# A decoder layer on one core: early score groups subtract earlier, VectorE evicts some queries, late rows are moved, and the last block takes other PSUM banks

## The chip, the cores and the metric

The kernel runs on one core of a Trainium2 chip. The metric is the device time of the whole program in microseconds; less is better. One execution was taken by the hardware profiler, and every view below is of that execution.

## The reference, cut to what matters

There are 16 sequences of 256 tokens with 256 features, all in float32 (4,096 token rows).

1. **First attention.** Rows are normalised, four heads of 64 features are multiplied with 256 fixed keys, the scores go through relu and square, and the result is multiplied with fixed values: `y = x + out`, then a layer norm of `x + y`.
2. **Cross attention.** 16 heads of 16 features attend within each sequence to 256 rows of a context. The logits have a bias that depends on a clipped difference of two scalars per row: `attn = q·k + ap_h * max(D,0) + an_h * min(D,0)`, with `D = clip(frac_k - frac_q, -0.2, 0.2)`. Softmax, values, an output projection, a residual, a layer norm.
3. **Feed-forward.** 256 to 1,024 to 256 features with relu, and a low-rank correction (rank 4) that one of eight experts adds, chosen by a gate. A residual and a last layer norm.

## The kernel before, in words

The order of all instructions is written out by hand (`manual_schedule`), and each engine runs its own instructions strictly in that order. The rows are held as 8 blocks of 512.

**First stage, up to about 259 us:** the first attention, block after block.

**Second stage, from about 259 to 840 us:** one loop over `n` from 0 to 65. Each `n` below 64 is a *group*: one sequence (batch `b = n // 4`) and four of its heads (`og = n % 4`). The work of a group is spread over three rounds of the loop. Its names and lines:

- `negative` (L588 on GpSimd, L593 on ScalarE) makes `an_h * dneg` for the four heads of group `n+1`, `count` of them on GpSimd and the others on ScalarE, into a tile `neg` (three buffers).
- `positive` (L600, ScalarE) writes `ap_h * dpos` into the four PSUM banks `ps_l`, and `logits` (L609, TensorE, 16 matmuls) adds `q·k` to them.
- `maxima` (L624, VectorE, eight instructions) adds `neg` and the bank, stores the sum in `neg` and keeps each row's maximum `mx`.
- `subtract` (L639) takes the maxima off: heads 0 and 1 on GpSimd, heads 2 and 3 on VectorE. Both read two SBUF tensors (`neg`, `mx`).
- in round `n+1`: `turned` (L649, TensorE transposes, four matmuls a head) and `exps` (L656, ScalarE), heads 0 and 1 first, then a *large piece*, then heads 2 and 3.
- in round `n+2`: `attend` (L665, TensorE) and, every second group, `keep` (L678, VectorE copies the bank `av`); after a batch's last group the sums and values leave by DMAs (L521, L529), are inverted (`invert`, L537, VectorE) and spread by DMAs (`spread`, L539, L547).

The large piece depends on `og`: 0 is `queries` of the next batch (L437, evicted at L447 by ScalarE), 1 is `project` of an older batch (L561, added at L570 by VectorE), 2 is `keys` (L457, evicted at L467 by VectorE and copied by eight DMAs, L473, into `kM`), 3 is `vals` (L479, evicted at L487 by VectorE into `vaug`) with a *small piece* behind heads 2 and 3: the transposes L424 of the batch after next.

`tile_b` hands out three PSUM banks in strict rotation to all of these: heads 0 to 3 of `turned`, the large piece, the small piece. So an allocation waits until the one three before it has been evicted.

From `n = 15` on (`FIRST`), the feed-forward of one block is laid into eight rounds (`part` 0 to 7, the block's `ff`). Part 0 turns the rows, part 1 has the matmuls of the gate (L764, copied at L772), parts 2 and 3 (`halved`) have half of the inner products each (L830, L842, relu at L849 on ScalarE and L853 on VectorE) and, in part 2, `route` (L783 to L799, VectorE), and parts 4 to 7 have the outer products (L860). Rounds 0 to 14 have no `ff`; they are called *early groups* here.

Before the change, `subtract` stands behind the eviction of the large piece:

```python
if older:
    older.keep()
...
step(large_piece)
...
if now and not halved:
    now.subtract((nc.gpsimd, nc.gpsimd if n == 0 else nc.vector))
```

The second half of the first attention's last block is finished in rounds 24 to 27: one `norm_out` (L249 on ScalarE, L379 on GpSimd) at the end of each.

**End, from about 840 us:** blocks `six` and `seven` of the feed-forward without groups beside them. `six.inner(1)` uses the four banks `ps_l` again, behind their relu of the first half (L849, L853).

Of the kernel before, what the change touches and what calls it, by code (L numbers as in the profile page):

```python
# [10 lines left out]
AF = mybir.ActivationFunctionType  # L11
ALU = mybir.AluOpType
AX = mybir.AxisListType

P = 128
# [6 lines left out]
def tile_decoder_layer(ctx: ExitStack, tc: tile.TileContext, a: dict, out: bass.AP):  # L22


    nc = tc.nc
    NTOK, C = a["x"].shape
    B, S = a["frac"].shape
    NT = NTOK // P
    NB = NTOK // 512
# [67 lines left out]
    bq_s = const.tile([P, CC], FP, name="bq_s")  # L97
# [10 lines left out]
    loraB = const.tile([P, F], FP, name="loraB")  # L108
# [278 lines left out]
    if True:  # L387
# [8 lines left out]
        class Batch:  # L396
# [33 lines left out]
                self.xT = p2.tile([P, CC, S], FP, tag="xT", bufs=1, name="xT")  # L430
                nc.scalar.copy(self.xT.rearrange("p c t -> p (c t)"), ps)

            def queries(self):
                ps = tile_b()
                for o in range(CC):
                    for c in range(CC):
                        nc.tensor.matmul(  # L437
                            ps[:, o * S : (o + 1) * S],
                            lhsT=wq[:, c, o * P : (o + 1) * P],
                            rhs=self.xT[:, c, :],  # L440
                            start=(c == 0),
                            stop=(c == CC - 1),
                        )
                yield
                self.qT = p2.tile([P, CC, S], FP, tag="qT", name="qT")
                for o in range(CC):
                    nc.scalar.activation(  # L447
                        self.qT[:, o, :], ps[:, o * S : (o + 1) * S], AF.Identity,
                        bias=bq_s[:, o : o + 1], scale=qscale,
                    )  # L450
# [236 lines left out]
        def pieces(n):  # L687

            b, og = divmod(n, 4)
            ahead, nxt, last, older = (  # L690
                batches[b + d] if 0 <= b + d < B else None for d in (2, 1, -1, -2)
            )
            if og == 0:
                return nxt and nxt.queries(), None, []
            later = nxt if nxt and nxt.b >= MADE else None
            if og == 1:
                return older and older.project(), None, [later and (lambda: later.clip("dneg"))]
            if og == 2:
                return nxt and nxt.keys(), None, [later and (lambda: later.clip("dpos"))]
            more = [ahead and ahead.load]  # L700
            if ahead:
                more.append(ahead.reload if ahead.b < MADE else ahead.fractions)
            return nxt and nxt.vals(), ahead and ahead.turned(), more
# [7 lines left out]
    if True:  # L711
        out_view = out.rearrange("(b j p) c -> b p j c", j=4, p=P)

        class Block:
# [99 lines left out]
                self.umT = pm.tile([P, 512], FP, tag="umT", bufs=1, name="umT")  # L814
                nc.scalar.copy(self.umT, ps)

            def inner(self, half, gs=range(4)):
                if half == 0 and 0 in gs:
                    if self.tb == NB - 1:
                        h0 = pm.tile([P, 4, 512], FP, tag="pT", name="hT0")  # L820
                        h1 = p2.tile([P, 4, 2, S], FP, tag="neg", bufs=3, name="hT1")
                        self.hT = [h0[:, g] for g in range(4)]
                        self.hT += [h1[:, g].rearrange("p j k -> p (j k)") for g in range(4)]
                    else:
                        h = pm.tile([P, FC, 512], FP, tag="hT", bufs=1, name="hT")
                        self.hT = [h[:, f] for f in range(FC)]
                for g in gs:
                    f = 4 * half + g
                    for c in range(CC):
                        nc.tensor.matmul(  # L830
                            banks[g],
                            lhsT=wi[:, c, f * P : (f + 1) * P],
                            rhs=self.xT[:, c, :],
                            start=(c == 0),
                            stop=False,
                        )

            def lora(self, half, scalar=(0, 2)):
                for g in range(4):
                    f = 4 * half + g  # L840
                    rows = slice(ER * g, ER * g + ER)
                    nc.tensor.matmul(  # L842
                        banks[g], lhsT=loraB[rows, f * P : (f + 1) * P], rhs=self.umT[rows, :],
                        start=False, stop=True,
                    )
                for g in range(4):
                    f = 4 * half + g
                    if g in scalar:
                        nc.scalar.activation(  # L849
                            self.hT[f], banks[g], AF.Relu, bias=wib[:, f : f + 1]  # L850
                        )
                    else:
                        nc.vector.tensor_scalar(  # L853
                            self.hT[f], banks[g], wib[:, f : f + 1], 0.0, ALU.add, ALU.max
                        )

            def outer(self, j, ps):
# [15 lines left out]
                nc.vector.tensor_tensor(rows, rows, ps[:, 0:C], ALU.add)  # L873
                row_stats(rows, self.mv[:, j, :])

            def finish(self, j):
                ps = tile_b()
                self.outer(j, ps)
                self.add(j, ps)

# [14 lines left out]
    with tc.manual_schedule():  # L895
# [15 lines left out]
        by = [None] * (NB + 1)  # L911
# [4 lines left out]
        for tb in range(NB):  # L916
            now = rows_in[tb]
# [29 lines left out]
            if tb + 1 < NB:  # L947
                nxt = rows_in[tb + 1]
# [50 lines left out]
        banks = [psL.tile([P, 512], FP, tag=f"L{g}", name=f"ps_l{g}") for g in range(4)]  # L999
# [8 lines left out]


        FUSED, FIRST = NB - 2, 15  # L1010
        six, seven = rows_out[NB - 2 :]
        rest = rows_in[NB - 1]
        rest.mv = const.tile([P, 4, 2], FP, name="mv_rest")
        for n in range(N + 2):
            now, nxt, last, older = (
                groups[n + d] if 0 <= n + d < N else None for d in (0, 1, -1, -2)
            )
            large_piece, small_piece, more = pieces(n)
            tb, part = divmod(n - FIRST, 8)
            ff = rows_out[tb] if 0 <= tb < FUSED or (tb == FUSED and part < 2) else None  # L1020
            halved = ff and part in (2, 3)
# [15 lines left out]
            if older and not halved and n != N:  # L1037
                older.attend()
            if nxt:
                nxt.negative(4 if 1 <= n < FIRST - 1 else 3)  # L1040
            if prep:
                prep.root()
            if done:
# [13 lines left out]
            if halved:  # L1057
                for g in range(2):
                    last.turned(g)
                    last.exps(g)  # L1060
                if part == 2:
                    ff.route()
                now.subtract((nc.gpsimd, nc.vector))
                if part == 2:
                    ff.biased()
                if done:
                    done.ready(newton(done.mv, done.near, 4))
                ff.inner(part - 2, range(0, 3))
                if part == 2:
                    ff.turn_um()  # L1070
                ff.inner(part - 2, range(3, 4))
                ff.lora(part - 2, scalar=(0,))
                for g in range(4):
                    nxt.positive(g)
                older.attend()
            else:
                if nxt:
                    nxt.positive(0)
                    nxt.positive(1)
                if last:  # L1080
                    last.turned(0)
                    last.exps(0)
                if nxt:
                    nxt.positive(2)
                if last:
                    last.turned(1)
                    last.exps(1)
                if n == N:
                    older.attend()
                if nxt and not (ff and part == 0):  # L1090
                    nxt.positive(3)
                if prep:
                    prep.rows()
            if older:
                older.keep()
            if n == 0:
# [18 lines left out]
            divided = batches[b - 2] if og == 0 and b >= 2 else None  # L1115
            if divided and ff:
                divided.divide()
            if now and not halved:
                now.subtract((nc.gpsimd, nc.gpsimd if n == 0 else nc.vector))
            if divided and not ff:  # L1120
                divided.divide()
            if done and not halved:
# [15 lines left out]
                    extra()  # L1138
            if 16 <= n < 20:
                row_stats(rest.y[:, n - 16, :], rest.mv[:, n - 16, :])  # L1140
            if 24 <= n < 28:
                rest.norm_out(by[NB], n - 24, n - 24, nc.gpsimd)

            tb, part = divmod(n - FIRST + 4, 8)
            if part < 3 and 0 <= tb <= FUSED:
# [13 lines left out]
        six.inner(0, range(3, 4))  # L1159
        six.lora(0)  # L1160
        end.divide()
        six.inner(1)
        step(add)
        step(add)
        six.lora(1)
        for j in range(2, 4):
            seven.measure(j)
        seven.norm()
        six.finish(0)
        six.finish(1)  # L1170
        seven.turn()
        seven.biased()
# [88 lines left out]
```

## Time and profile before

| what | value |
|---|---|
| median of 3 runs | 914.74 us (914.54 to 915.02) |
| the profiled execution's own time | 914.93 us |
| its span in the profile | 913.1 us |
| TensorE busy | 892.4 us (98%) |
| VectorE busy | 707.7 us (78%) |
| ScalarE busy | 584.2 us (64%) |
| GpSimd busy | 379.5 us (42%) |
| granted TensorE clock | 1.0 |

How to read it: an engine's busy time is the union of its instructions' times; the ends of matmuls are modelled. The execution's own time is 1.8 us more than the span. A line of the timeline has the start, the duration, the engine, the source line, the operation, what it writes and reads, how many instructions were merged, and in brackets how long the engine stood idle before it and what ended that. Idle gaps under 0.15 us are not listed.

### The profile page before, as it was taken

The numbers are of one execution on the slowest core, as the hardware profiler recorded it, in microseconds if no ns is written. First come the engines' busy times: TensorE is split into PE (matmuls) and PEld (weight loads), VectorE is DVE, ScalarE is ACT, GpSimd is POOL, SyncE is SP. The second block draws the span as 40 slices with busy tenths as digits, with TensorE's granted clock in tenths as the row PEclk, the third lists the DMA queues.
The fourth block names the chain that finished last, engine by engine and source line by source line (L and its number), as shares of the span: only waits on it lengthen the run. The fifth ranks groups of instructions, "written<-read, shape, count | busy, mean of one in ns | idle before, by whom it ended". The sixth has DMA issues, their size and how long they took to land.

```text
span 913.1 us, 19025 instructions
## 1 busy us (share of the span) xinstructions
PE 892.4 (98%) x6910; PEld 541.6 (59%) x6910; DVE 707.7 (78%) x1968; ACT 584.2 (64%) x977; POOL 379.5 (42%) x369
## 2 busy tenths in 40 slices
PE   6999999999999999999999999999999999999997
PEld 2333333333356776577658757865875686586555
DVE  5788899889878998778777877777787787678443
ACT  4757877787687879466666856665685567556111
POOL 1002312231469996434635543463454336244010
PEclk9999999999999999999999999999999999999999
DMA  5411011100001222010111202011120201111001
GB/s 137 146 36 35 30 36 41 65 1 2 3 11 50 70 71 56 13 42 21 35 43 39 52 13 66 18 37 41 40 52 14 65 17 40 41 27 45 23 1 47
DMA packets 44190, 37.01 MB, mean 41 GB/s; under 512 B 14912, under 2 KB 40000, under 8 KB 44096
## 3 DMA queue, kind: packets, MB, share of 16 engines
q1 hardware_dynamic: 43536, 35.52, 14.0%
q8 instruction: 55, 0.90, 0.4%
q14 instruction: 39, 0.32, 0.1%
q10 hardware_dynamic: 560, 0.26, 0.1%
HBM read 21.07 MB, written 6.03 MB: 30 GB/s over the span
## 4 chain that ended last, share of the span: by engine, by line
PE 56%; ACT 4%; DVE 1%; issue 1%; ACTq 0%; DVEq 0%
PE ps_b L860 12%; PE ps_l L830 12%; PE ps_b L649 9%; PE ps_l L609 6%; PE ps_v L665 5%; PE ps_b L561 3%; PE ps_b L457 2%; PE ps_b L479 2%; PE ps_l L842 2%; ACT ps_l L600 2%; ACT pT L656 1%; PE ps_b L437 1%; PE ps_b L749 1%; ACT qT L447 1%; DVE neg L624 1%
## 5 line engine op out<-in xcount | busy, mean ns | idle before, releaser
L588 POOL TENSOR_SCALAR neg<-dneg,aneg,delta 128x512 f32<-128x512 f32 x205 | 175.7, 869 | 211.2 <-ACT pT L656 185.8
L624 DVE CUSTOM_DVE_ANT_0 neg<-ps_l,neg 128x256 f32<-128x256 f32 x512 | 181.6, 420 | 43.0 <-PE ps_l L609 39.8
L600 ACT ACTIVATE ps_l<-dpos,apos_d 128x512 f32<-128x512 f32 x256 | 173.1, 686 | 34.5 <-DVE mx L624 30.5
L656 ACT ACTIVATE pT<-ps_b 128x512 f32<-128x512 f32 x256 | 143.3, 590 | 59.1 <-PE ps_b L649 57.4
L324 DVE TENSOR_TENSOR pr<-r 128x1024 f32<-128x1024 f32 x128 | 155.5, 1255 | 32.4 <-ACT r L322 32.1
L322 ACT ACTIVATE r<-ps_a 128x1024 f32<-128x1024 f32 x128 | 126.5, 1022 | 59.1 <-PE ps_a L314 33.9
L649 PE MATMUL ps_b<-ident,neg 128*128 128x128 f32 x1024 | 140.3, 278 | 4.0 <-ACT pT L656 2.4
L649 PEld LDWEIGHTS ps_b<-ident,neg 128*128 128x128 f32 x1024 | 112.9, 140 | 41.9 <-issue 15.3
L639 POOL TENSOR_TENSOR neg<-neg,mx 128x1024 f32<-128x1024 f32 x65 | 124.3, 1914 | 30.0 <-DVE mx L624 24.0
L314 PE MATMUL ps_a<-xnT,kT 64*64 64x512 f32 x1024 | 124.2, 601 | 0.0
L334 PE MATMUL ps_v<-pr,vv 64*64 64x512 f32 x1024 | 123.5, 593 | 0.3
L860 PE MATMUL ps_b<-wof,hT 128*128 128x256 f32 x512 | 115.8, 380 | 0.0
L830 PE MATMUL ps_l<-xt,wi 128*128 128x512 f32 x256 | 115.0, 596 | 0.8 <-ACT hT L849 0.8
L860 PEld LDWEIGHTS ps_b<-wof,hT 128*128 128x128 f32 x512 | 96.4, 190 | 16.0 <-issue 2.3
L639 DVE TENSOR_TENSOR neg<-neg,mx 128x1024 f32<-128x1024 f32 x63 | 90.9, 1443 | 0.3
L349 POOL TENSOR_TENSOR xt<-xt,half 128x512 f32<-128x512 f32 x15 | 23.7, 1583 | 141.0 <-ACT half L348 141.0
L334 PEld LDWEIGHTS ps_v<-pr,vv 64*64 64x64 f32 x1024 | 38.1, 132 | 70.7 <-issue 43.7
L314 PEld LDWEIGHTS ps_a<-xnT,kT 64*64 64x64 f32 x1024 | 38.1, 135 | 67.9 <-issue 56.2
L830 PEld LDWEIGHTS ps_l<-xt,wi 128*128 128x128 f32 x256 | 46.8, 190 | 52.0 <-issue 45.8
L609 PE MATMUL ps_l<-kM,qT 32*128 32x256 f32 x1024 | 74.8, 401 | 0.4 <-ACT ps_l L600 0.4
L665 PE MATMUL ps_v<-pT,vaug 128*32 128x256 f32 x1024 | 69.8, 385 | 0.8 <-ACT pT L656 0.8
L853 DVE TENSOR_SCALAR hT<-ps_l,wib 128x512 f32<-128x512 f32 x44 | 30.5, 745 | 42.8 <-PE ps_l L842 42.8
(107 smaller groups left out, 966.9 us busy)
## 6 DMA issues: line engine op xcount, KB each, us to landing
cT<-in_ctxT SPq DMA_DIRECT2D x16, 256.0 KB
kM<-keys SPq DMA_DIRECT2D x128, 32.0 KB
v<-raw SPq DMA_DIRECT2D x128, 32.0 KB
invs<-rows SPq DMA_DIRECT2D x128, 32.0 KB
x<-in_x SPq DMA_DIRECT2D x7, 512.0 KB
out<-x SPq DMA_DIRECT2D x7, 512.0 KB
frow<-in_frac SPq DMA_DIRECT2D x16, 128.0 KB
wi<-in_wiT SPq DMA_DIRECT2D x1, 1024.0 KB
```

The costliest lines, as they stand in the source:

```text
L314: nc.tensor.matmul(sc[64 * k : 64 * k + 64, h, :], lhsT=kT[64 * h : 64 * h + 64, q, hf * P + 64 * k : hf * P + 64 * k + 64], rhs=self.xnT[ ...
L324: nc.vector.tensor_tensor(pr, r, r, ALU.mult)
L334: nc.tensor.matmul(self.acc[k][64 * h : 64 * h + 64, :], lhsT=vv[64 * k : 64 * k + 64, hf, 64 * q : 64 * q + 64], rhs=pr[64 * k : 64 * k + ...
L588: nc.gpsimd.tensor_scalar(self.neg[:, g], self.batch.dneg, aneg[:, h : h + 1], delta, ALU.mult, ALU.mult,)
L600: nc.scalar.activation(banks[g], self.batch.dpos.rearrange("p j k -> p (j k)"), AF.Copy, scale=apos_d[:, h : h + 1],)
L609: nc.tensor.matmul(banks[g][:, j * S : (j + 1) * S], lhsT=self.batch.qT[rows, self.o, j * P : (j + 1) * P], rhs=self.batch.kM[rows, self.i ...
L624: nc.vector.tensor_tensor_reduce(out=self.t[:, g, j, :], in0=banks[g][:, j * S : (j + 1) * S], in1=self.neg[:, g, j, :], scale=1.0, scalar ...
L639: eng.tensor_tensor(rows, rows, top.to_broadcast([P, 4, S]), ALU.subtract)
L649: nc.tensor.transpose(ps[:, k * S + j * P : k * S + (j + 1) * P], self.t[:, g, j, k * P : (k + 1) * P], ident,)
L656: nc.scalar.activation(self.pT[:, g, :], self.ps[g], AF.Exp)
L830: nc.tensor.matmul(banks[g], lhsT=wi[:, c, f * P : (f + 1) * P], rhs=self.xT[:, c, :], start=(c == 0), stop=False,)
L860: nc.tensor.matmul(ps[:, 0:C], lhsT=self.hT[f][:, j * P : (j + 1) * P], rhs=wof[:, f, :], start=(f == 0), stop=(f == FC - 1),)
```

## The change

- Rounds 0 to 14: `subtract` stands directly behind `maxima` and what follows it in the round's first half, ahead of `keep`, of `invert` and of the large piece's eviction. From round 15 on it stays where it was.
- `negative`: in rounds 1 and 2 GpSimd makes three heads and ScalarE one (before: four and none); in parts 0 and 1 GpSimd makes four (before: three and one).
- `queries` of rounds 16, 24, ... 56 are evicted by VectorE instead of ScalarE. These rounds are part 1.
- The four `norm_out` stand at the ends of rounds 24, 27, 28 and 29.
- At the end `six.inner(1)` takes two of its four banks from `tile_b`, and `six.finish(0)` takes the bank `V`.

```diff
-            def queries(self):
+            def queries(self, vector=False):
...
                 for o in range(CC):
+                    if vector:
+                        nc.vector.tensor_scalar(
+                            self.qT[:, o, :], ps[:, o * S : (o + 1) * S], qscale,
+                            bq_s[:, o : o + 1], ALU.mult, ALU.add,
+                        )
+                        continue
                     nc.scalar.activation(
...
-                return nxt and nxt.queries(), None, []
+                return nxt and nxt.queries(n > 15 and n % 8 == 0), None, []
...
-            def inner(self, half, gs=range(4)):
+            def inner(self, half, gs=range(4), own=()):
+
+                if 0 in gs:
+                    self.banks = list(banks)
...
+                    if g in own:
+                        self.banks[g] = tile_b()
...
-            def finish(self, j):
-                ps = tile_b()
+            def finish(self, j, ps=None):
+                ps = ps or tile_b()
...
+        LATE = 24, 27, 28, 29
...
-                nxt.negative(4 if 1 <= n < FIRST - 1 else 3)
+                nxt.negative(4 if 3 <= n < FIRST - 1 or (ff and part < 2) else 3)
...
+            if now and not halved and not ff:
+                now.subtract((nc.gpsimd, nc.gpsimd if n == 0 else nc.vector))
             if older:
                 older.keep()
...
-            if now and not halved:
-                now.subtract((nc.gpsimd, nc.gpsimd if n == 0 else nc.vector))
+            if now and not halved and ff:
+                now.subtract((nc.gpsimd, nc.vector))
...
-            if 24 <= n < 28:
-                rest.norm_out(by[NB], n - 24, n - 24, nc.gpsimd)
+            if n in LATE:
+                j = LATE.index(n)
+                rest.norm_out(by[NB], j, j, nc.gpsimd)
...
-        six.inner(1)
+        six.inner(1, own=(0, 1))
...
-        six.finish(0)
+        six.finish(0, tile_v())
```

(In `inner` and `lora`, `banks[g]` becomes `self.banks[g]`.)

More of the change, by code (lines that the diff above doesn't have):

```diff
@@ L828, in inner @@
                     f = 4 * half + g
+                    if g in own:
+                        self.banks[g] = tile_b()
                     for c in range(CC):
                         nc.tensor.matmul(
-                            banks[g],
+                            self.banks[g],
                             lhsT=wi[:, c, f * P : (f + 1) * P],
@@ L842, in lora @@
                     nc.tensor.matmul(
-                        banks[g], lhsT=loraB[rows, f * P : (f + 1) * P], rhs=self.umT[rows, :],
+                        self.banks[g], lhsT=loraB[rows, f * P : (f + 1) * P], rhs=self.umT[rows, :],
                         start=False, stop=True,
@@ L849, in lora @@
                         nc.scalar.activation(
-                            self.hT[f], banks[g], AF.Relu, bias=wib[:, f : f + 1]
+                            self.hT[f], self.banks[g], AF.Relu, bias=wib[:, f : f + 1]
                         )
@@ L853, in lora @@
                         nc.vector.tensor_scalar(
-                            self.hT[f], banks[g], wib[:, f : f + 1], 0.0, ALU.add, ALU.max
+                            self.hT[f], self.banks[g], wib[:, f : f + 1], 0.0, ALU.add, ALU.max
                         )
```

## The prediction

> **What bounds the kernel now.** I read the busy times first, then TensorE's waits, early groups and the rest apart, then the timeline of single rounds.
>
> ```profile
> PE 892.4 (98%) x6910; PEld 541.6 (59%) x6910; DVE 707.7 (78%) x1968; ACT 584.2 (64%) x977; POOL 379.5 (42%) x369
> ```
>
> TensorE (PE) stands idle for 913.1 - 892.4 = 20.7 us. Its waits are short lists (total us, times, longest), first for 250 to 300 us, then from 335 us on; before 250 us there is only the start, 8.6 us, which the change doesn't touch.
>
> ```profile
> PE ps_b L649 <- ACT pT L656: 1.6, 4, 0.5
> PE ps_l L609 <- ACT ps_l L600: 0.4, 1, 0.4
> ```
>
> ```profile
> PE ps_b L649 <- ACT qT L447: 1.4, 6, 0.2
> PE ps_b L649 <- ACT pT L656: 0.9, 2, 0.4
> PE ps_v L665 <- ACT pT L656: 0.8, 1, 0.8
> PE ps_l L830 <- ACT hT L849: 0.8, 1, 0.8
> PE ps_b L809 <- DVE um L799: 0.5, 1, 0.5
> ```
>
> That is 6.4 us, and all that the edits could win. Everywhere else PE runs without a gap, so whatever makes PE wait anew is added in full. So I ask of each edit whom it makes late. Round 7 (og 3, `vals`) decides:
>
> ```profile
> 300.77 1.15 PE L609 MATMUL ps_l<-kM,qT 32*128 32x256 f32 x16
> 301.01 3.89 POOL L588 TENSOR_SCALAR neg<-dneg,aneg,delta 128x512 f32<-128x512 f32 x4 [0.51 <-POOL neg L639]
> 304.82 0.69 DVE L678 COPY raw<-ps_v 128x512 f32<-128x512 f32 x1
> 304.86 1.89 POOL L639 TENSOR_TENSOR neg<-neg,mx 128x1024 f32<-128x1024 f32 x1
> 305.70 0.69 DVE L487 COPY vaug<-ps_b 128x512 f32<-128x512 f32 x1 [0.20 <-PE ps_b L479]
> 306.31 1.52 DVE L639 TENSOR_TENSOR neg<-neg,mx 128x1024 f32<-128x1024 f32 x1
> 306.47 0.63 PE L424 MATMUL ps_b<-ident,hid 128*128 128x128 f32 x4
> ```
>
> Write L for the start of a round's logits (300.77). Maxima end at L + 4.13 (304.90). `keep` and the eviction of `vals` run while GpSimd subtracts; the eviction ends at 306.39, and L424, which by the rotation takes that bank, starts 0.08 us later, at L + 5.70. The logits of round 8 are queued behind L424. Round 8 (og 0) has nothing between maxima and subtract, so it already is what the change makes of every early group:
>
> ```profile
> 310.69 1.88 POOL L639 TENSOR_TENSOR neg<-neg,mx 128x1024 f32<-128x1024 f32 x1
> 311.21 2.45 DVE L639 TENSOR_TENSOR neg<-neg,mx 128x1024 f32<-128x1024 f32 x1
> ```
>
> VectorE's subtract takes 2.45 us here, 2.26 in round 4 and 2.44 in round 12. Clear of GpSimd's it takes 1.22 (round 15, at 356.87). It ends 1.08 us behind GpSimd's (313.66 against 312.57): it waited.
>
> **The change, part by part.**
>
> **The early subtract.** GpSimd's four negatives may start at L + 0.25 (301.01; 313.08 in round 9, L 312.83) and last 0.76 each, 3.0 together; only the first was stretched, by the previous subtract of VectorE. So GpSimd subtracts from L + 3.3 to L + 5.2, ahead of VectorE, which asks at L + 4.13 and ends at L + 5.2 + 1.08 = L + 6.3. If the previous subtract ends after L + 0.25, this is up to 0.15 later. `keep` and the eviction of `vals` follow, 2 x 0.69 - 0.08 = 1.3: L + 7.6, where L424 wanted L + 5.7. Queued behind that wait on PE are L424 and the next logits; behind the logits, all else. Cost 1.9 us in rounds 7 and 11 each. In round 3 VectorE's previous subtract ends near 276.8, the negatives at 279.75, GpSimd's subtract at 281.6, VectorE's at 282.7, the eviction at 284.0; L424 stood at 282.59, behind 0.53 us of idle that this takes up: 1.4 us. Sum 5.2. If the two subtracts did not meet, the eviction would end at L + 4.13 + 1.22 + 1.3 = L + 6.6, and the cost would be 0.9, 0.9 and 0.2: 2.0. If GpSimd began only at the maxima's end, as at 304.86, it is 2.6, 2.6 and 2.0: 7.2. I take 5.2, since rounds 4, 8 and 12 show the meeting each time.
>
> [...]
>
> **The same edit in the other early groups.** Round 13 (`project`): subtract to L + 6.3, `keep` and L570 to L + 7.5, then two row statistics (1.16 from 343.77 to 344.93): L + 8.6. The next logits come at L + 5.85 and maxima could start 1.29 behind them, L + 7.1: 1.5 late, where they were 0.5 late before (344.89 against 343.12 + 1.29); the exps and transposes hang on them, so PE loses 1.0. Round 9, without statistics: 0.3. Rounds 6, 10 and 14 (`keys`): at most 0.3 late, covered by the stalls of 7 and 11 or by the small vector operations of 14; I take 0. Their eight DMAs to `kM`, and the sums, values and inverses that SP issues, start up to 2.2 us later; the first half of `kM` of round 10 was there about 1.7 us before the logits that read it (330.74), and round 11's stall adds 1.9: covered. Without that stall it costs 0.5. Won back: round 4's wait (0.25) and round 13's (0.44), since after a stall VectorE is on time. Early groups in all: 5.2 + 1.0 + 0.3 - 0.7 = 5.8.
>
> **Negatives.** Rounds 1 and 2 take 0.75 us each off GpSimd. ScalarE's extra 0.72 lies in an idle 1.8 us in round 1; in round 2 it has 0.31 idle, so positives come 0.4 late and PE waits 0.25 (inside the 1.4 of round 3). In parts 0 and 1 GpSimd has idle time of 0.8 to 3.3 us before its instructions (358.28, 361.38, 438.71), so one more is hidden; without it, 0.75. ScalarE's 0.75 less is no one's wait.
>
> **Queries on VectorE** (rounds 16 to 56, six times). Head 3's transposes wait for the bank of the queries:
>
> ```profile
> 445.63 0.66 PE L649 MATMUL ps_b<-ident,neg 128*128 128x128 f32 x4 [0.23 <-ACT qT L447]
> ```
>
> VectorE can evict when the matmuls end (443.8, its maxima end at 442.95): two at 0.44 to 0.49 (L467, same shape and source), done by 444.3 instead of 445.57. The wait goes: -1.4 in all. Behind it on VectorE, divide and subtract end 0.7 us later; then VectorE has 2.1 us idle before the next maxima, so that is hidden. Bounds: -1.4 and 0.
>
> **Late rows.** The one at the end of round 24 stays, and it is its GpSimd addition (447.48) that is queued ahead of round 25's negatives and its subtract (450.43), which `route` meets (L791, 1.66 instead of some 0.35). So the 0.5 us at L809 stays. The other three move to rounds with idle GpSimd and ScalarE: 0. Bounds: -0.85 (round 25 lasts 15.35 between logits, round 33 14.50) and 0.
>
> **Other banks at the end.**
>
> ```profile
> 851.04 7.13 PE L830 MATMUL ps_l<-xt,wi 128*128 128x512 f32 x16 [0.76 <-ACT hT L849]
> ```
>
> The wait goes, the rotation's banks are free (evicted by 844.4), and banks 2 and 3 are free (851.8) before their turn, 3.4 us in: -0.8.
>
> **Sum:** +5.8 - 1.4 - 0.8 = +3.6. From the profiled 914.93 (span 913.1) 918.5; the profiled run lies 0.2 above the median, so 918.3 against 914.74.
>
> **The rivals.**
>
> *Faster: the eviction of `vals` is not awaited.* If L424's bank were another one, late evictions would cost nothing, and the early waits of rounds 3, 4, 13 and 14 (0.4 each but for round 4) would go: -1.5 - 1.4 - 0.8 = -3.7, 911.0. It decides if L424 starts before L487 ends. Against it: the rotation counted out (L424 is three allocations behind `vals`), and L424 starting 0.08 us behind the eviction.
>
> *No change: the subtracts don't meet.* VectorE gets through first, the `vals` rounds cost 2.0, the rest of the early groups nets -0.3 (0.7 won, some 0.4 lost in rounds 9 and 13): 2.0 - 0.3 - 2.2 = -0.5, 914.2; with round 25 gaining, 913.4. It decides if VectorE's subtract lasts under 1.4 us in rounds 5 to 13. For it: round 1, where VectorE went ahead of the fourth negative, which then took 1.73 instead of 0.77. Against it: GpSimd is ready 0.8 us earlier.
>
> *Worse: the chain of SP.* If `kM` lands late in rounds 8 and 12 as well (2.2 us later against 2.3 and 1.7 spare) and the subtracts meet as at 304.86, it is 7.2 + 1.3 + 0.5 - 0.7 - 2.2 = +6.1, 920.8. It decides if PE waits for a DMA there.
>
> **How the numbers follow.** Forecast 0.60, worse 0.13, no change 0.14, faster 0.13. What differs by less than 0.2% (1.8 us) I call the same, about what this measurement can tell. Slower is forecast and worse, 0.73; faster is the first rival and the end of the second, 0.14; same 0.13. The range leaves out about a tenth at each end: 912.6 to 921.0; the forecast's own range is 916.5 to 919.5 (its bounds of 0.85 at round 25, and 0.5 to 1 on the `vals` rounds).
>
> **What would show it.** Right: PE waits at L424 for `vaug` in rounds 3, 7 and 11, 1.4 to 2 us each; VectorE's subtract near 2.3 us in the early groups; no wait for `qT`, none at the end's L830; the wait at L809 still there. Wrong: no listed wait for `vaug`, or subtracts of 1.2 us. A span from first logits to round 15's logits that is shorter than 89.7 us (259.73 to 349.46) would overturn the forecast.

## The result, and the profile after

| | before | after |
|---|---|---|
| median of six runs | 914.64 us (913.71 to 915.02) | 918.00 us (916.14 to 918.40) |
| ratio | | 1.0034, 95% interval 1.0023 to 1.0045 |
| the profiled execution | 914.93 us, span 913.1 | 918.4 us, span 916.6 |

The change made the kernel 3.4 us slower; 918.3 had been predicted. The engines' busy times of the changed kernel:

```profile
PE 892.8 (97%) x6910; PEld 542.2 (59%) x6910; DVE 712.2 (78%) x1980; ACT 573.9 (63%) x955; POOL 380.5 (42%) x379
```

TensorE did the same work in the same busy time (892.4 before), so the 3.5 us by which the span grew are idle time, and matmuls that ran slowly (below). TensorE's waits, whole run (total us, times, longest):

```profile
PE ps_b L424 <- DVE vaug L493: 5.1, 3, 1.8
PE ps_b L655 <- ACT pT L662: 2.3, 5, 0.8
...
PE ps_b L815 <- DVE um L805: 0.5, 1, 0.5
```

The first line is new: three waits for the eviction of `vals` (L493; L487 before). The lines for `qT` (1.4) and `hT` (0.8) are gone, and the wait at `um` stayed. Round 7 in the timeline of the changed kernel; L645 is `subtract`, L684 `keep`:

```profile
304.99 1.89 POOL L645 TENSOR_TENSOR neg<-neg,mx 128x1024 f32<-128x1024 f32 x1
305.88 2.09 DVE L645 TENSOR_TENSOR neg<-neg,mx 128x1024 f32<-128x1024 f32 x1
307.89 0.68 DVE L684 COPY raw<-ps_v 128x512 f32<-128x512 f32 x1
308.49 0.68 DVE L493 COPY vaug<-ps_b 128x512 f32<-128x512 f32 x1
309.22 0.66 PE L424 MATMUL ps_b<-ident,hid 128*128 128x128 f32 x4 [1.65 <-DVE vaug L493]
```

VectorE's subtract asks at 305.88 and ends at 307.97, which is 1.09 behind the end of GpSimd's (306.88). `keep` and the eviction follow, and L424 starts 0.05 behind the eviction's end. This round's logits began at 301.59, so the eviction ends 7.58 behind them: the prediction said 7.6.

At the end, the inner products of the second half now start with a bank of the rotation, straight behind the low-rank part (L853), where 0.76 us of waiting had been:

```profile
853.43 1.14 PE L853 MATMUL ps_l<-umT,loraB 32*128 32x512 f32 x8
854.50 3.70 PE L841 MATMUL ps_b<-xt,wi 128*128 128x512 f32 x8
```

One thing was not foreseen. Busy time in three stretches of 3.41 us (columns: stretch, length, busy us and count of PE, PEld, DVE, ACT, POOL, then the granted TensorE clock, the DMA share and GB/s):

```profile
306.93:310.35 3.42, 1.77 (x18) 1.34 (x22) 2.23 (x3) 1.95 (x4) 2.60 (x4) 1.00 0.19 49
310.35:313.76 3.41, 3.41 (x31) 1.49 (x24) 2.21 (x13) 1.49 (x3) 1.09 (x2) 0.50 0.25 63
334.24:337.65 3.41, 1.82 (x20) 1.40 (x24) 2.58 (x5) 2.00 (x4) 2.70 (x4) 1.00 0.20 48
```

Behind the wait of round 7 the granted clock is 0.50 for 3.41 us, and round 8's matmuls take longer (the logits 1.62 us instead of 1.15). Behind the wait of round 11 (last line) it stays at 1.00.

Where the time went, from the starts of the logits in the two traces (after less before; change within the stretch):

| stretch | us | predicted |
|---|---|---|
| up to the first logits | -0.54 | 0 |
| rounds 3, 7, 11 (`vals`) | +1.21, +1.95, +1.77 = +4.93 | +5.2 |
| round 8 (the clock) | +1.49 | 0 |
| the other early rounds | +1.04 | +0.6 |
| rounds 16, 24, ... 56 (the *gate rounds*) | 6 x -0.45 = -2.70 | -1.4 |
| the other rounds from 15 on | +0.07 | 0 |
| the end | -0.83 | -0.8 |
| sum | +3.46 | +3.6 |

The prediction's test, first logits to round 15's logits, gave 97.19 us against 89.73: longer, as forecast.

The table explains the profiled execution and not all six. Their spans are 916.6, 916.2, 915.2, 915.1, 914.4 and 914.9 us. The granted clock has a mean of 0.997 in the first two, and of 0.999 or 1.0 in the others. Two of the others took 918.03 and 918.01 us all the same, 2.9 and 3.1 us more than their spans, where the profiled one took 1.8 more. No run shows what that extra time is.

### The profile page after: what moved, and what is told of

Its sections match the earlier page's. It is cut to its first block, busy times and chain, and to the rows that moved or that the text cites. A ratio compares the mean times of both kernels' runs of the same rounds, so it can differ in the third digit from the quotient of the medians.

```text
span 916.6 us, 18997 instructions
## 1 busy us (share of the span) xinstructions
PE 892.8 (97%) x6910; PEld 542.2 (59%) x6910; DVE 712.2 (78%) x1980; ACT 573.9 (63%) x955; POOL 380.5 (42%) x379
## 4 chain that ended last, share of the span: by engine, by line
PE 84%; DVE 9%; ACT 3%; issue 2%; DMA 1%; SPq 1%; DVEq 0%; ACTq 0%
PE ps_b L871 11%; PE ps_l L841 11%; PE ps_b L655 11%; PE ps_v L334 10%; PE ps_a L314 10%; PE ps_l L615 7%; PE ps_v L671 6%; PE ps_b L567 3%; DVE pr L324 3%; PE ps_b L437 2%; PE ps_b L485 2%; PE ps_b L463 2%; DVE neg L630 2%; PE ps_l L853 2%; PE ps_b L295 1%
## 5 line engine op out<-in xcount | busy, mean ns | idle before, releaser
L645 POOL TENSOR_TENSOR neg<-neg,mx 128x1024 f32<-128x1024 f32 x65 | 124.4, 1914 | 30.5 <-DVE mx L630 29.7
L314 PE MATMUL ps_a<-xnT,kT 64*64 64x512 f32 x1024 | 123.5, 598 | 0.3 <-ACT r L322 0.3
L871 PE MATMUL ps_b<-wof,hT 128*128 128x256 f32 x496 | 112.3, 380 | 0.0
L841 PE MATMUL ps_l<-xt,wi 128*128 128x512 f32 x248 | 111.5, 595 | 0.0
L871 PEld LDWEIGHTS ps_b<-wof,hT 128*128 128x128 f32 x496 | 93.4, 190 | 15.0 <-issue 1.5
L645 DVE TENSOR_TENSOR neg<-neg,mx 128x1024 f32<-128x1024 f32 x63 | 93.9, 1491 | 0.7
L314 PEld LDWEIGHTS ps_a<-xnT,kT 64*64 64x64 f32 x1024 | 37.9, 134 | 67.8 <-issue 56.2
```

What stands on the lines that cost most here:

```text
L314: nc.tensor.matmul(sc[64 * k : 64 * k + 64, h, :], lhsT=kT[64 * h : 64 * h + 64, q, hf * P + 64 * k : hf * P + 64 * k + 64], rhs=self.xnT[ ...
L645: eng.tensor_tensor(rows, rows, top.to_broadcast([P, 4, S]), ALU.subtract)
L841: nc.tensor.matmul(self.banks[g], lhsT=wi[:, c, f * P : (f + 1) * P], rhs=self.xT[:, c, :], start=(c == 0), stop=False,)
L871: nc.tensor.matmul(ps[:, 0:C], lhsT=self.hT[f][:, j * P : (j + 1) * P], rhs=wof[:, f, :], start=(f == 0), stop=(f == FC - 1),)
```

## The experiments

Every ratio is to the kernel before, measured beside it on the same chip; its medians there were 914.94, 914.92 and 914.84. "Stage" is the time from the first logits to round 15's logits in the profiled execution (before: 89.73). It is the finest measure here: the start of the run alone shifts the first logits by up to 1 us either way between executions, and the stage leaves that out.

| label | median us | ratio, 95% interval | stage us |
|---|---|---|---|
| late_subtract | 910.27 | 0.9951, 0.9938 to 0.9963 | 89.00 |
| early_subtract_only | 920.23 | 1.0057, 1.0045 to 1.0070 | 94.90 |
| vals_first | 913.36 | 0.9983, 0.9974 to 0.9992 | 91.04 |
| queries_only | 911.64 | 0.9969, 0.9956 to 0.9981 | 89.72 |
| negatives_only | 913.95 | 0.9991, 0.9981 to 1.0000 | 89.09 |
| other_bank | 915.10 | 1.0006, 0.9997 to 1.0015 | 93.59 |
| one_input | 927.17 | 1.0137, 1.0120 to 1.0154 | 105.62 |
| late_one_input | 926.50 | 1.0127, 1.0112 to 1.0142 | 104.52 |
| two_pieces | 915.05 | 1.0003, 0.9993 to 1.0012 | 93.98 |
| late_two_pieces | 911.13 | 0.9963, 0.9951 to 0.9976 | 89.86 |
| stall_steps | 918.67 (one run) | | 96.10 |
| after_again | 920.15 (one run) | | 98.27 |

### Which edit costs, and which gain

**late_subtract.** The early subtract undone, all else kept:

```diff
-            if now and not halved and not ff:
-                now.subtract((nc.gpsimd, nc.gpsimd if n == 0 else nc.vector))
...
-            if now and not halved and ff:
-                now.subtract((nc.gpsimd, nc.vector))
+            if now and not halved:
+                now.subtract((nc.gpsimd, nc.gpsimd if n == 0 else nc.vector))
```

> The changed kernel with one edit undone: in rounds 0 to 14 subtract stands behind the large piece's eviction again. The other four edits stay. Theory (the early subtract costs all the loss, the rest only gains): the three waits of PE at L424 for vaug go, the granted clock stays at 1.0 near 310 us, the stage from first logits to round 15's logits is 89.7 us again, and the gate rounds and the end keep their gains, 6 x 0.45 = 2.7 and 0.8: 914.6 - 3.5 = 911.1 us. If the gate rounds are worth only the listed idle of 0.23 each, as predicted, and round 2's three negatives cost 0.25: 914.6 - 1.4 - 0.8 + 0.25 = 912.7. Rival (the loss comes from the negatives or from the moved rows, not from the subtract): it stays near 918.

Measured 910.27, better than both kernels. The waits at L424 and the clock's fall are gone (mean clock 0.999). Its gain by place: -0.73 in the stage, -2.70 in the gate rounds, -0.82 at the end. The -0.73 was not expected; it is round 3, 0.84 shorter, less round 2, 0.11 longer.

**early_subtract_only.** The kernel before, with that one move:

```diff
+            if now and not halved and not ff:
+                now.subtract((nc.gpsimd, nc.gpsimd if n == 0 else nc.vector))
             if older:
                 older.keep()
```

> The kernel before with the early subtract alone. Theory (GpSimd's and VectorE's subtracts exclude each other, so vals' eviction is late and PE waits at L424): waits for vaug of 1.4 to 2 us in rounds 3, 7 and 11, VectorE's subtract near 2 us, first logits to round 15's logits 95.7 us, and 914.6 + 6.0 = 920.6 us; with a fall of the granted clock in round 8, as in the profile of the changed kernel, 97.2 and 922.1. If that fall belongs to the wait, it comes again here; if it is chance, it need not. Rival (the subtracts don't meet; the loss came from the fewer negatives on GpSimd in rounds 1 and 2 that shifted the phase): 916.5 or less.

Measured 920.23, stage +5.17. The waits in rounds 7 and 11 are there (+1.94, +1.76), but round 3 costs only +0.19, where the changed kernel has +1.21. Round 3 in this kernel's timeline:

```profile
280.39 1.28 DVE L639 TENSOR_TENSOR neg<-neg,mx 128x1024 f32<-128x1024 f32 x1
...
282.29 1.89 POOL L639 TENSOR_TENSOR neg<-neg,mx 128x1024 f32<-128x1024 f32 x1
282.93 0.66 PE L424 MATMUL ps_b<-ident,hid 128*128 128x128 f32 x4 [0.83 <-DVE vaug L487]
```

Here VectorE went ahead of GpSimd's subtract and needed 1.28 us. GpSimd came later, since in this kernel it still makes four negatives in round 2. In the changed kernel it makes three, is ready sooner, goes first, and VectorE takes 2.26. Two edits that look unrelated decide together who goes first. The clock stayed at 1.0 behind round 7's wait of 1.65 us: round 8's logits took 1.15.

**vals_first.** The changed kernel, with the subtract behind the eviction again where the large piece is `vals`:

```diff
-            if now and not halved and not ff:
+            if now and not halved and not ff and og != 3:
...
-            if now and not halved and ff:
-                now.subtract((nc.gpsimd, nc.vector))
+            if now and not halved and (ff or og == 3):
+                now.subtract((nc.gpsimd, nc.gpsimd if n == 0 else nc.vector))
```

> The changed kernel, but in early groups with og 3 (rounds 3, 7, 11) subtract stands behind the eviction of vals again; in the other early groups it stays early. Theory (only the eviction of vals is awaited by PE): the three waits at L424 go (5.0 us by the listed idle) and, if the clock's fall near 310 us hangs on the wait of round 7, that goes too (1.5); what is left of the early edit is +1.0 (round 13 with its row statistics), so 914.6 + 1.0 - 2.7 - 0.8 = 912.1 us, first logits to round 15's logits 90.8. Rival (the early subtracts of og 0 to 2 push the later evictions by themselves, through queries and keys): waits stay at other pieces, 915 or more.

Measured 913.36 (912.1 expected), stage +1.31. No wait at L424, no fall of the clock (mean 0.999). What is left: +0.94 in round 9, +0.44 and +0.68 in rounds 13 and 14, and -0.84 won in round 3. The early move costs in the `project` rounds too, and the most that it wins in any round is 0.15 (round 12).

**queries_only.**

```diff
-                return nxt and nxt.queries(), None, []
+                return nxt and nxt.queries(n > 15 and n % 8 == 0), None, []
```

> The kernel before with one edit: queries of rounds 16, 24, ... 56 are evicted by VectorE. Theory A (the wait of PE for qT is really 0.45 each, since the listed idle begins only at the modelled end of the matmuls before it): 914.6 - 2.7 = 911.9 us, each of the six rounds 0.45 shorter. Theory B (0.23 each, the listed idle, as predicted; the rest of the gain in the changed kernel came from the negatives that left ScalarE in the same rounds): 914.6 - 1.4 = 913.2.

Measured 911.64; each of the six rounds is 0.45 shorter, so theory A. Round 16 in its timeline, evicted by VectorE (L448), then the transposes of heads 2 and 3 and the logits:

```profile
364.12 1.00 DVE L448 TENSOR_SCALAR qT<-ps_b,qscale,bq_s 128x256 f32<-128x256 f32 x2 [0.80 <-PE ps_b L437]
365.02 1.09 PE L655 MATMUL ps_b<-ident,neg 128*128 128x128 f32 x8
366.04 1.15 PE L615 MATMUL ps_l<-kM,qT 32*128 32x256 f32 x16
```

From the first of these transposes to the logits it is 1.02 us. In the kernel before:

```profile
364.31 0.66 PE L649 MATMUL ps_b<-ident,neg 128*128 128x128 f32 x4
365.20 0.66 PE L649 MATMUL ps_b<-ident,neg 128*128 128x128 f32 x4 [0.23 <-ACT qT L447]
365.78 1.15 PE L609 MATMUL ps_l<-kM,qT 32*128 32x256 f32 x16
```

There it was 365.78 - 364.31 = 1.47, with 0.23 listed as idle. The other 0.22 sat in the modelled ends: a group of four transposes that is followed by a wait lasts 0.66, eight in a row 1.09, and 2 x 0.66 - 1.09 = 0.23.

**negatives_only.** The kernel before, with the edit of `negative` alone:

```diff
-                nxt.negative(4 if 1 <= n < FIRST - 1 else 3)
+                nxt.negative(4 if 3 <= n < FIRST - 1 or (ff and part < 2) else 3)
```

> The kernel before with one edit: in rounds 1 and 2 GpSimd makes three negatives and ScalarE one; in parts 0 and 1 GpSimd makes all four. Theory, from the kernel with the early subtract undone: in round 2 VectorE's subtract no longer runs beside GpSimd's (1.2 instead of 2.2 us), the maxima of round 3 come a microsecond sooner, and rounds 0 to 3 are 0.7 to 0.85 us shorter; parts 0 and 1 change nothing. First logits to round 15's logits 88.9 instead of 89.7, the rest as before; 914.9 - 0.8 = 914.1. By the prediction: rounds 1 and 2 cost 0.25 instead, 915.2. Rival (the gate rounds' 0.45 each come from these negatives in part): rounds 16, 24 to 56 get shorter as well.

Measured 913.95; the interval touches 1, so the trace has to speak: round 3 is 0.83 shorter, round 2 is 0.11 longer, and the gate rounds are as before. Round 2 in the timeline of the kernel before, then of this one:

```profile
275.30 1.89 POOL L639 TENSOR_TENSOR neg<-neg,mx 128x1024 f32<-128x1024 f32 x1
276.04 2.23 DVE L639 TENSOR_TENSOR neg<-neg,mx 128x1024 f32<-128x1024 f32 x1
```

```profile
272.82 1.90 POOL L639 TENSOR_TENSOR neg<-neg,mx 128x1024 f32<-128x1024 f32 x1
274.95 1.22 DVE L639 TENSOR_TENSOR neg<-neg,mx 128x1024 f32<-128x1024 f32 x1
```

With one negative less, GpSimd has ended (274.72) before VectorE asks. So this edit belongs with the late subtract, where it keeps the two apart; with the early one it makes them meet.

**other_bank.** The changed kernel, with the rotation moved on by one ahead of the small piece:

```diff
+                if turns and self.b < 5:
+                    turns[0] += 1
                 ps = tile_b()
```

> The changed kernel, but the rotation of the three banks is moved on by one ahead of each small piece of the early batches; as built, L424 then takes a bank that ScalarE evicts in rounds 3 and 7, and still the bank of vals in round 11. It is the prediction's first rival made true in two of three rounds. Theory (PE waits for the eviction of vals only because of the bank): no wait at L424 in rounds 3 and 7 although vals is evicted as late as before, no fall of the clock near 310 us, and the wait of 1.6 us in round 11 stays; early groups cost 1.3 + 1.8 = 3.1 instead of 7.5 us (1.3 is what the kernel with vals evicted first still loses), and the time is 918.0 - 4.4 = 913.6 us. Rival (the next round's transposes or attend wait for the same late eviction or for the bank taken instead): waits of the same size at L655 or L671 in rounds 4 and 8, 917 to 918.

Lines are two further on than in the changed kernel: L426 is L424 there, and L495 is L493. Rounds 7 and 11:

```profile
307.85 0.65 PE L426 MATMUL ps_b<-ident,hid 128*128 128x128 f32 x4 [0.44 <-ACT pT L664]
308.32 0.68 DVE L495 COPY vaug<-ps_b 128x512 f32<-128x512 f32 x1
...
333.94 0.66 PE L426 MATMUL ps_b<-ident,hid 128*128 128x128 f32 x4 [1.59 <-DVE vaug L495]
```

In round 7 the matmuls start ahead of the late eviction; in round 11, with the bank of `vals`, they wait 1.59. So PE waits for the eviction because of the bank and for nothing else. The size fell short (915.1 against 913.6; the stage lost 3.86 against 3.1): the bank taken instead costs waits of 0.44 for ScalarE in rounds 3 and 7, and round 10 is 0.48 longer.

### What VectorE waits for

**one_input** and **late_one_input.** GpSimd's half of the subtract in four instructions with one SBUF tensor each:

```diff
+                    if single and g == 0:
+                        for h in range(2):
+                            for j in range(2):
+                                nc.gpsimd.tensor_scalar(
+                                    self.t[:, h, j, :], self.t[:, h, j, :],
+                                    self.mx[:, h, j : j + 1], None, ALU.subtract,
+                                )
+                        continue
```

> The changed kernel, but from round 1 on GpSimd subtracts with four instructions tensor_scalar (128x256 each, the maximum as a scalar of each partition) in place of one tensor_tensor of 128x1024 with two SBUF tensors; same results. Theory (VectorE waits only while GpSimd runs an instruction with two SBUF tensors): VectorE's subtract takes 1.2 to 1.4 us in all early groups, the waits at L424 fall from 1.6 to 1.8 to about 0.9 each (the prediction's rival without a meeting), no fall of the clock near 310 us; early groups cost some +3.0 instead of +7.5, and the time is about 914.9 + 3.0 - 3.5 = 914.4 us. Rival (any two instructions of GpSimd and VectorE that run at once slow each other, as a shared memory would): VectorE's subtract stays at 1.8 to 2.4 us, the waits too, 917 to 918.

> The kernel with the early subtract undone (910.3 us), and in rounds 1 to 14 GpSimd subtracts with four tensor_scalar of one SBUF tensor instead of one tensor_tensor. Theory: VectorE's subtract takes 1.2 to 1.4 us in every early group (there 1.2 to 2.4), maxima of the next group start earlier, and PE's waits for pT in these rounds (2.0 us in five waits) fall by half or more: 909 us, first logits to round 15's logits 88 us. Rival A (any two instructions at once slow each other): VectorE's subtract as before, no gain, 910.3. Rival B (GpSimd's four are slower together than the one of 1.89 us, so heads 0 and 1 come late at the transposes): new waits of PE for neg, 911 or more.

Both are far slower, by much more than any theory said: one such instruction of 128x256 takes 0.92 us, the four 3.6 instead of 1.89. PE waits 10.1 and 10.8 us for `neg` (rival B of the second), and the clock fell in both (mean 0.996 and 0.995). The theory of the two SBUF tensors fell too. Round 3 of one_input, where the GpSimd instruction at work is a negative with one SBUF tensor:

```profile
279.74 0.77 POOL L594 TENSOR_SCALAR neg<-dneg,aneg,delta 128x512 f32<-128x512 f32 x1
280.23 1.34 DVE L653 TENSOR_TENSOR neg<-neg,mx 128x1024 f32<-128x1024 f32 x1
```

VectorE ends at 281.57, 1.06 behind that negative's end (280.51); the next negative, recorded from 280.49 on, then took 1.73 instead of 0.77.

Beside the new subtracts of 0.92 us, though, VectorE lost less. Round 13 of one_input:

```profile
353.75 0.92 POOL L646 TENSOR_SCALAR neg<-neg,mx 128x256 f32<-128x256 f32 x1
353.97 1.32 DVE L653 TENSOR_TENSOR neg<-neg,mx 128x1024 f32<-128x1024 f32 x1
```

VectorE asked 0.22 behind the other's start and ended only 0.62 behind its end (354.67). In the eleven meetings of this kind in the two runs it is 0.62 to 0.95. The next expectation starts from 1.07 to 1.08 behind whichever GpSimd instruction ran; that holds for the negatives and not for these. Why is open.

**two_pieces** and **late_two_pieces.** GpSimd's half as two `tensor_tensor` of one head each:

```diff
+                    count = 2 // pieces if g == 0 else 2
+                    for h in range(g, g + 2, count):
```

> The changed kernel, but from round 1 on GpSimd's subtract in early groups is two tensor_tensor of 128x512 (one head each) instead of one of 128x1024. Theory, mended after the run with four tensor_scalar (VectorE's subtract there ended 1.07 to 1.08 us behind the end of whichever GpSimd instruction ran when it asked, with one SBUF tensor or two): the two engines exclude each other one instruction at a time, so VectorE waits only for the first piece, 0.95 us less; its subtract takes 1.2 to 1.6 us, the waits at L424 fall from 1.6 to 1.8 to about 0.7 to 0.9, there is no fall of the clock near 310 us, and the time is 918.0 - 3 x 0.95 - 1.5 = 913.7 us. Rival (VectorE waits until GpSimd's queue of ready work is empty): nothing changes, 917 to 918, or GpSimd's second piece, now behind VectorE's, makes PE wait for neg at the transposes of head 1.

> The kernel with the early subtract undone (910.3 us), and in rounds 1 to 14 GpSimd's subtract as two tensor_tensor of 128x512. Theory: VectorE's subtract takes at most 1.6 us (there up to 2.45, in rounds 8 and 12), the maxima of rounds 4, 9 and 13 start up to 0.9 sooner, and of PE's 2.0 us of waits for pT in these rounds 0.5 to 1 goes: 909.5 us. Rival (GpSimd's second piece and the negatives behind it come 1.2 us later wherever VectorE gets in between, so maxima wait for neg): same or worse, 910.3 to 911.

Round 7 of two_pieces:

```profile
305.12 1.03 POOL L647 TENSOR_TENSOR neg<-neg,mx 128x512 f32<-128x512 f32 x1
305.73 1.51 DVE L647 TENSOR_TENSOR neg<-neg,mx 128x1024 f32<-128x1024 f32 x1
```

VectorE ends 1.09 behind the first piece (306.15) and ahead of the second, so the mended theory holds for these pieces: VectorE waits for the one instruction that is at work. In rounds 5 and 13 it asked some 0.1 us before the first piece's end and still went behind the second (2.2 us). Round 7 costs 1.25 instead of 1.95, there is no fall of the clock (mean 0.999), and 915.05 is 3 us better than the changed kernel, though it misses the 913.7 expected: in round 11 VectorE asked early in the first piece and lost most of it (1.56 instead of 1.77). late_two_pieces missed: 911.13, not below 910.27. VectorE's longest subtract fell from 2.45 to 2.17 us, but others grew, and no wait for `pT` went away (2.2 us in six).

### What a wait does to the clock

**stall_steps.** late_subtract with longer `keep` in three rounds:

```diff
-                older.keep()
+                older.keep({3: 4, 7: 5, 11: 7}.get(n, 1))
```

> The kernel with the early subtract undone, and in rounds 3, 7 and 11 keep copies the same bank 3, 4 and 6 times more (0.6 to 0.7 us each on VectorE, ahead of the eviction of vals), so that PE stands at L424 for about 1.8, 2.4 and 3.6 us; same results. It asks what a wait does to the granted clock. In the changed kernel the records show a clock of 0.5 from 310.35 to 313.76, behind a wait of 1.65 us, and none behind 1.82 and 1.59. Theory A (a stretch of 3.41 us, counted on from the first rise of the clock, with PE busy for less than some 1.8 us makes the next stretch slow): at least the waits of 2.4 and 3.6 are each followed by 3.41 us at 0.5, and each costs 1.5 us beyond the wait. Theory B (only a stretch that is idle throughout does that, and the fall near 310 us had another cause): the clock stays at 1.0.

The waits did not come as planned: in these rounds L424 started ahead of the end of the eviction of `vals` (in round 3 at 283.13, the eviction ended at 283.84), so it had another bank, and it waited 0.4 to 0.9 us for ScalarE. The delay showed in other waits, two of them of 1.1 and 1.2 us. One stretch had PE busy for 1.78 us (339.26 to 342.67), and the next had a clock of 0.5. That agrees with theory A and goes against B, but the waits of 2.4 and 3.6 us that were to test A never came.

**after_again.** The changed kernel, unchanged.

> The changed kernel once more, for a second profile. The waits at L424 in rounds 3, 7 and 11 come again (they are set by the order of instructions), each within 0.1 us of 1.8, 1.6 and 1.6. Theory (the stretches of 3.41 us by which the clock is set stand elsewhere against the waits in each execution): the clock may stay at 1.0 this time, and then first logits to round 15's logits take 97.2 - 1.5 = 95.7 us, or it may fall behind another of the three waits, and then 97.2. Rival (the fall belongs to round 7 and is no matter of chance): a clock of 0.5 behind round 7's wait again.

The three waits came again (1.83, 1.67, 1.60), and the clock fell twice, behind rounds 7 and 11:

```profile
307.46:310.87 3.41, 1.75 (x18) 1.17 (x20) 2.42 (x3) 1.93 (x5) 2.56 (x5) 1.00 0.22 55
310.87:314.28 3.41, 3.41 (x33) 1.43 (x26) 1.82 (x11) 1.29 (x3) 0.92 (x2) 0.50 0.23 53
334.77:338.18 3.41, 1.81 (x18) 1.33 (x20) 2.78 (x5) 1.99 (x5) 2.50 (x4) 1.00 0.21 51
338.18:341.59 3.41, 3.41 (x31) 1.45 (x27) 2.12 (x13) 1.44 (x3) 1.07 (x2) 0.50 0.25 77
```

Round 8 was +1.48, round 12 +1.33 where the first profile had -0.15. Round 11's wait is the same in both; only the stretches lie differently, with PE busy for 1.81 us here and 1.82 there. So neither "round 7 alone" nor "one fall" holds. The six executions of the result fit: the two with a mean clock of 0.997 have the longest spans (916.6 and 916.2, the others 914.4 to 915.2), and this one, with 0.996, has 918.4.

## Why the prediction was right, point by point

**The `vals` rounds.** The step holds in mechanism and size: 1.82, 1.65 and 1.59 us of waiting, +4.93 for 5.2. The shared bank is the cause (other_bank), and evicting `vals` first is the remedy (vals_first). Had the subtracts not met, so that VectorE's took its 1.22 us of round 15, the same sum would have given 2.0; the rows of rounds 4, 8 and 12 (2.26, 2.45 and 2.44 us) were the better guide.

**Round 3 was right for a reason not given.** Its 1.4 stood on VectorE going second. That is true only with the three negatives of rounds 1 and 2. With four, the move alone costs 0.19 there, so this term came out by luck.

**Negatives: the step that failed.** "Rounds 1 and 2 take 0.75 us each off GpSimd" was priced by idle time alone, at nothing or +0.25. Alone the edit wins 0.83 in round 3 and loses 0.11 in round 2. The question of who goes first, put to the subtract, was not put to the negatives. Alone the two edits sum to +0.19 - 0.83 = -0.64 in round 3, together they give +1.21.

**The other early groups.** +1.04 for a net +0.6. Round 14 lost 1.40, not 1.0: its maxima start 3.17 behind the logits (351.81 against 348.64), before it was 1.77, and the whole difference reached PE. The mis-sized part is how late they start: 1.9 behind their earliest time of 1.29, where 1.5 was predicted, since VectorE's subtract of round 13 ended 6.71 behind that round's logits (349.46 against 342.75) and not 6.3. The 0.5 by which they had been late before was rightly taken off. Of the 0.7 to be won back, round 13 gave 0.54 and round 4 nothing. Round 9's 0.3 did not show (-0.05 there, +0.23 in round 10), and it is 0.94 where no stall precedes it (vals_first).

**Queries: a mis-sized term.** 0.45 each, not 0.23; the listed idle is what the modelled ends of the matmuls leave over. The interval of -1.4 to 0 left the true -2.7 out. With it falls the reading that the listed 6.4 us are all that the edits could win.

**Late rows, the end.** Both right: the wait at L815 stayed and rounds 25 to 29 moved by less than 0.1; the end won 0.83. The late rows were not run alone.

**Not in the sum at all:** the clock, +1.49 in the profiled execution, from nothing to some 3 in others. In the profiled execution the total came out close because the clock and the larger gain at the gates, +1.49 and -1.3, nearly cancel. In the four executions of the result whose mean clock shows no fall, the same account gives +2.0 in the span; that the median of all six is 918.00, beside the predicted 918.3, owes to two falls and to the two executions with 3 us outside their span. The direction follows from the mechanism; so close a number is luck.

**The rivals.** *The subtracts don't meet* fell: 1.7 to 2.45 us in rounds 5 to 13. *The chain of SP* fell: PE waits for no DMA in rounds 8 and 12. *The eviction is not awaited* fell with the three waits at L424; other_bank makes it true in two rounds, and even so the early groups lose 3.9 us.

## What to carry to other kernels

When two engines exclude each other, moving either one's work changes who goes first, so an edit on one must be priced together with every edit on the other; here two edits that alone cost 0.19 and win 0.83 in round 3 cost 1.21 there together. Where an engine hands back a buffer that the bottleneck needs, put that eviction ahead of work that can be blocked (vals_first: 913.36 us, where the changed kernel takes 918.00). Undo a mixed change edit by edit: four of the five edits here were gains, or nothing, and without the fifth the kernel runs in 910.27 us, 0.49% below the one before.

## What the runs showed of the hardware

**VectorE and GpSimd take turns, mostly by whole instructions.** VectorE's `tensor_tensor` of 128x1024 with two SBUF tensors takes 1.22 us clear of GpSimd. Where it asked while a `tensor_tensor` or a negative was at work on GpSimd, it ended 1.07 to 1.09 us behind the end of that one, in all 54 meetings in the profiles of the kernel before and of the changed kernel; in two_pieces it was 1.09 (round 7), and 1.06 behind the negative of one_input (round 3). The 54 leave out where it asked within the last 0.12 us: then it lost nothing (1.22 us, at 443.65 in the changed kernel), or went behind the next one (2.2 us, rounds 5 and 13 of two_pieces). The reverse was seen too: a negative that takes 0.77 us took 1.73 where it met VectorE's subtract (round 3 of one_input). The eleven meetings with the 0.92 us `tensor_scalar` (0.62 to 0.95, in one_input and late_one_input) don't fit; why is open.

**The clock can fall behind a wait of 1.6 us.** It changes in stretches of 3.41 us: the two falls of after_again last 3.41 each and begin 27.31 us apart, 8 times that; in the first profile of the changed kernel the fall begins 296.96 us behind the clock's rise at the start (310.35 against 13.39, where matmuls of L314 go from 1.06 to 0.59 us), 87 times that. Up to round 15, six such stretches were each followed by one at 0.5, with PE busy for 1.21 and 1.56 us (one_input), 1.75 and 1.81 (after_again), 1.77 (changed kernel) and 1.78 (stall_steps). Two in the changed kernel were not, with 1.82 (round 11) and 1.87 (round 3), nor was any with 2.0 or more in the first profile of that kernel or in the kernel before. In late_one_input the matmuls ran slowly from about 302.5 us on: those of `keys` (L463) took 3.62 us instead of 1.89, and in the 3.41 us ahead of it PE was busy for about 1.9, an estimate from the timeline. At the end of the program even the six are no guide; after_again again:

```profile
911.62:915.03 3.41, 1.41 (x7) 0.90 (x5) 1.88 (x8) 0.50 (x2) 0.00 (x0) 1.00 0.11 38
915.03:918.44 3.41, 0.00 (x0) 0.00 (x0) 0.72 (x3) 0.00 (x0) 0.00 (x0) 1.00 0.12 41
```

Here a stretch with 1.41 us of outer products is followed by one at 1.00. Each of the three falls in the changed kernel's two profiles cost 1.48 or 1.49 us. A stretch that was half idle sufficed for a fall (1.75 us busy of 3.41). By which measure of activity the chip decides stays open: the busy time used here has modelled ends, and neither the case at 1.9 nor the one at 1.41 fits a single bound.

**GpSimd's `tensor_scalar` with a column of maxima** took 0.92 us for 128x256, the negatives (two scalars) 0.76 for 128x512. Why was not tried.

**The banks of `tile_b` are not always in strict order.** In stall_steps L424 started 0.7 us ahead of the end of the eviction of `vals`, so it had another bank, with no edit to the rotation. The code fixes only that every third allocation takes one bank of its own; the two between take from a pool of two buffers. So the strict rotation told ahead of the prediction fits the waits at L424 in the two kernels compared here and is no rule; what it hands out has to be read from the built kernel each time.
